# A two-layer metaformer on one core: the tiles of layer 0's experts in source order, their results stored from GpSimd's queue, and two products moved from GpSimd to VectorE

## The chip, the cores and the metric

The kernel runs on one core of a Trainium2 chip. Its engines work side by side, each through its own queue of instructions in order: TensorE (PE in the profile; its weight loads, PEld, overlap its matmuls), VectorE (DVE), ScalarE (ACT), GpSimd (POOL) and SyncE (SP), which here issues most of the DMA transfers. A profile also lists the clock that TensorE was granted. The metric is the device time of one execution in microseconds (us), as the median of several. The kernel before has three: 4149.68, 4160.04 and 4175.90 us.

## The reference

The input x is 4 images of 256 channels by 32 × 32 places, in float32. Two layers follow each other; each has a mixing half and a mixture of experts, added to x.

```
# layer 0
x = x + attention(norm_channels(x))      # 8 heads, a computed top-k, softmax, 3x3 convolution, projection
t = tokens(x)                            # 4096 tokens of 256
n = norm(t)
t = t + n + sum over the 2 chosen of 8 experts of  weight * (gelu(n @ w1[e] + b1[e]) @ w2[e] + b2[e])
# layer 1
f = norm_channels(x)
delta = softplus(f @ W_delta + b_delta);  Bm, Cm = f @ W_B, f @ W_C
h[l] = exp(delta * A) * h[l-1] + delta * f * Bm       # 16 states, in four directions over the image
x = x + (sum over the directions of (h . Cm) + f * D) / 4
t = t + the 2 chosen of 8 experts, hidden size 1024, a norm with the expert's own gain before each
```

w1 and w2 of layer 0 are 256 × 256 for each expert. The change touches layer 0's experts and the preparation (delta and delta·f) for the scans of layer 1.

## The kernel before

**Stages.** The program goes through attention (to 1905 us of the profiled execution), the norm and routing of layer 0 (to 2045), the tiles of layer 0's experts (to 2276), the scans of layer 1 (2283 to 3561), the tiles of layer 1's experts (to 4111) and the output. A planner inside the framework orders the instructions of a stage on each engine, unless the source is put under `tc.manual_schedule()`, in which case they stay in source order.

**Routing.** For each image, tokens are normed, the two experts chosen, and GpSimd scatters every token twice into rows of a DRAM tensor, slots_x0, so that each expert's rows stand together in blocks of 256. A list of 36 blocks (USUAL) covers the usual case; a branch on `more_tiles` does the rest, and the profiled execution did not take it.

**Tiles of layer 0** (`tile0`, L1480 and following). One tile is one block of 256 rows. SP reads the number of the block and of the expert into registers and loads xs (the rows, L1517), w1 and w2. VectorE copies the expert's biases out of a table that lies in SBUF (b1e L1521, b2e L1523) and computes best and wt, the choice and the weight of each row (L1525 to L1528). PE transposes the rows into tp (L1532), VectorE copies them to xe (L1534). PE multiplies into hp (L1539, two halves), ACT applies the gelu to each half, giving hid (L1540), PE multiplies into yp (L1544), and VectorE adds b2e, giving ys (L1546). For each half of ys, ACT scales it (L1548) and VectorE adds the token itself (L1549). SP's queue stores ys, 256 KB, into slots_y0 in DRAM (L1550). tp and yp have one PSUM buffer each, hp has two; ys has four buffers in SBUF.

**What goes beside the tiles.** Two chains of steps are woven in between the calls of tile0, four steps ahead of each tile: from tile 15 (FIRST) `whole(0)` and then the preparation of image 0 (`Prep.steps`), from tile 23 (SECOND) `whole(1)`. `whole(b)` gathers image b's rows out of slots_y0: GpSimd issues 16 indirect transfers (`fetched`, L1451), two to a step, 8 that write and 8 that add. After eight empty steps, `completed` transposes the rows on PE (op, L1464) and VectorE adds them to x (L1467). Because the gathers can read any row of slots_y0, and the stores write rows of it whose numbers are known only in registers, the framework makes each wait for those ahead of it in the program. Images 2 and 3 are completed later, beside the scans.

**Preparation for the scans** (`Prep.steps`). For one image: the mean over channels on PE (L1341), xm = x − mean on VectorE (L1344), its square on ACT (L1345), the variance on PE (L1353), 1/sqrt with a power on GpSimd (L1359) and four small VectorE steps to refine it (L1361 to L1364), a matmul that spreads it over the partitions (L1371), xm times it on VectorE (L1375), the matmuls for Bm and Cm (L1381) and for delta (L1407). Then the softplus for each half of the channels: Relu, Abs and Exp on ACT, three VectorE steps (L1419 to L1421), Ln on ACT (L1430), a VectorE step (L1434) and a GpSimd addition (L1435). `rest` follows with dx = delta·xm on GpSimd (L1393) and x + xm·D on VectorE (L1394). L1435 and L1393 are each issued four times for an image, on 128 × 512 elements in SBUF. Prep 0 runs beside the tiles of layer 0; Preps 1 to 3 run beside the scans.

**Scans.** 128 turns (4 images, 2 halves of the channels, 16 states). In each turn, VectorE does three scans of 128 × 1024 (L1671 forward, L1680 backward, both with decays da in PSUM; L1697 over columns, with all operands in SBUF), one small scan (L1686) and two products with Cm (L1707). GpSimd does uu = dx·Bm (L1658), a small difference (L1676) and a third product, da_c (L1691). ACT computes the decays and a flipped copy of uu, and PE sums the directions (L1666, L1701, L1708).

Of the kernel before, what the change touches and what calls it, by code (L numbers as in the profile page):

```python
# [11 lines left out]
F32 = mybir.dt.float32  # L12
# [9 lines left out]
P = 128  # L22
# [39 lines left out]
def metaformer(ctx: ExitStack, tc: tile.TileContext, t: dict, out: bass.AP):  # L62
# [86 lines left out]
    with ExitStack() as st:  # L149
# [68 lines left out]
        class Group:  # L218


            def __init__(self, b, g):
                self.b, self.g = b, g
# [1099 lines left out]
    class Prep:  # L1322
# [9 lines left out]
        def steps(self, room, psum, tag):  # L1332
# [57 lines left out]
            def rest(c):  # L1390
                for h in range(NHALF):
                    cols = ts(h, HALF)
                    nc.gpsimd.tensor_tensor(self.dx[:, c, cols], self.delta[:, c, cols], xm[:, c, cols], ALU.mult)  # L1393
                    nc.vector.scalar_tensor_tensor(x[b][:, c, cols], xm[:, c, cols], dsk[:, c : c + 1],  # L1394
                                                   x[b][:, c, cols], ALU.mult, ALU.add)
                    yield
                    yield

            behind = iter(())
            for c in range(CT):  # L1400
# [31 lines left out]
                for h in range(NHALF):  # L1432
                    dd = self.delta[:, c, ts(h, HALF)]
                    nc.vector.scalar_tensor_tensor(dd, sp[:, h], -0.5, dd, ALU.mult, ALU.add)  # L1434
                    nc.gpsimd.tensor_tensor(dd, dd, sp[:, 2 + h], ALU.add)  # L1435
                yield
                yield
                behind = rest(c)
# [34 lines left out]

    with ExitStack() as st:
        wp = st.enter_context(tc.tile_pool(name="m0_w", bufs=1))
        pb = st.enter_context(tc.tile_pool(name="m0_b", bufs=2))
# [4 lines left out]
        b1 = load(wp, "b1_0", [P, E, CT])  # L1481
        b2 = wp.tile([P, E, C], F32, tag="b2_0", name="b2_0")
        nc.sync.dma_start(b2, t["b2_0"].rearrange("e d -> (e d)").partition_broadcast(P).rearrange(
            "p (e d) -> p e d", e=E))
        tokens = [wp.tile([P, NT, W0], F32, tag=f"tok{b}", name=f"tok{b}") for b in range(B)]
        scattered = nc.alloc_semaphore("scattered")
        for b in range(B):
            d = pb.tile([P, CT, L], F32, tag="d", name="d")
            here = slot0[:, :, ts(b, NT)]
            for _ in norm(b, 0, tokens[b], pb, ps_n, "t", "t", d):  # L1490
                pass
            for _ in route(b, 0, tokens[b], here, wp.tile([P, 2560], F32, tag="numbers", name="numbers"), ps_n, "t"):
                pass

            with tc.tile_critical(name=f"scatter{b}", no_gpsimd_drain=True):
                for n in range(NT):
                    for k in range(2):
                        nc.gpsimd.indirect_dma_start(
                            out=slots_x0, out_offset=bass.IndirectOffsetOnAxis(ap=here[:, k, n : n + 1], axis=0),
                            in_=tokens[b][:, n], in_offset=None).then_inc(scattered, 16)  # L1500
                nc.gpsimd.wait_ge(scattered, 16 * 2 * NT * (b + 1))
                if b == B - 1:
                    nc.clear_and_free_semaphores([scattered])

        blocks_x, blocks_y = (a.rearrange("(k a p) c -> k p a c", a=T // P, p=P) for a in (slots_x0, slots_y0))

        def tile0(i):
            def register(k, most, engines):
                return nc.values_load(every.which[0:1, k, i : i + 1], engines=engines, min_val=0, max_val=most,
                                      skip_runtime_bounds_check_because="the minimum with that of a count")  # L1510

            block = register(1, E * BLOCKS, [mybir.EngineType.SP])
            xs = pb.tile([P, T // P, W0], F32, tag="xs", name="xs", bufs=4)
            nc.sync.dma_start(xs, blocks_x[bass.ds(block, 1)].rearrange("o p a c -> p (o a) c"))
            e = register(0, E - 1, [mybir.EngineType.SP, mybir.EngineType.DVE])
            w1 = pb.tile([P, CT, C], F32, tag="w1", name="w1", bufs=3)
            nc.sync.dma_start(w1, t["w1_0"][bass.ds(e, 1)].rearrange("o (c p) f -> p (o c) f", p=P))  # L1517
            w2 = pb.tile([P, CT, C], F32, tag="w2", name="w2", bufs=3)
            nc.sync.dma_start(w2, t["w2_0"][bass.ds(e, 1)].rearrange("o (c p) f -> p (o c) f", p=P))
            b1e = pb.tile([P, CT], F32, tag="b1e", name="b1e")  # L1520
            nc.vector.tensor_copy(b1e, b1[:, bass.ds(e, 1)].rearrange("p o c -> p (o c)"))  # L1521
            b2e = pb.tile([P, C], F32, tag="b2e", name="b2e")
            nc.vector.tensor_copy(b2e, b2[:, bass.ds(e, 1)].rearrange("p o d -> p (o d)"))  # L1523
            best = pb.tile([P, T // P], F32, tag="best", name="best")
            nc.vector.tensor_scalar(best, xs[:, :, C], every.expert[:, i : i + 1], None, ALU.is_equal)  # L1525
            wt = pb.tile([P, T // P], F32, tag="wt", name="wt")
            nc.vector.tensor_tensor(wt, best, xs[:, :, C + 1], ALU.mult)
            nc.vector.tensor_tensor(wt, wt, xs[:, :, C + 2], ALU.add)  # L1528
            tp = ps1.tile([P, CT, T], F32, tag="tp", name="tp")
            for a in range(T // P):  # L1530
                for c in range(CT):
                    nc.tensor.transpose(tp[:, c, ts(a, P)], xs[:, a, ts(c, P)], ident)  # L1532
            xe = pb.tile([P, CT, T], F32, tag="xe", name="xe")
            nc.vector.tensor_copy(xe, tp)  # L1534
            hp = ps_h.tile([P, CT, T], F32, tag="hp", name="hp")
            hid = pb.tile([P, CT, T], F32, tag="hid", name="hid")
            for f in range(CT):
                for c in range(CT):
                    nc.tensor.matmul(hp[:, f], w1[:, c, ts(f, P)], xe[:, c], start=(c == 0), stop=(c == CT - 1))  # L1539
                nc.scalar.activation(hid[:, f], hp[:, f], AF.Gelu, bias=b1e[:, f : f + 1])  # L1540
            yp = ps1.tile([P, T // P, C], F32, tag="yp", name="yp")
            for a in range(T // P):
                for f in range(CT):
                    nc.tensor.matmul(yp[:, a], hid[:, f, ts(a, P)], w2[:, f, :], start=(f == 0), stop=(f == CT - 1))  # L1544
            ys = pb.tile([P, T // P, C], F32, tag="ys", name="ys", bufs=4)
            nc.vector.tensor_tensor(ys, yp, b2e.unsqueeze(1).to_broadcast([P, T // P, C]), ALU.add)  # L1546
            for a in range(T // P):
                nc.scalar.mul(ys[:, a], ys[:, a], wt[:, a : a + 1])  # L1548
                nc.vector.scalar_tensor_tensor(ys[:, a], xs[:, a, :C], best[:, a : a + 1], ys[:, a], ALU.mult, ALU.add)  # L1549
# [9 lines left out]
        more_tiles = nc.values_load(extra[0:1, 0:1], min_val=0, max_val=1,  # L1559
                                    skip_runtime_bounds_check_because="a comparison gives 0 or 1")  # L1560
        with tc.If(more_tiles > 0):
            for i in range(USUAL, NTILE):
                tile0(i)

        def whole(b):
            y = [pb.tile([P, 4, C], F32, tag=f"y{h}", name="y", bufs=1) for h in range(NHALF)]
            yield from fetched(b, y, range(NHALF), 2)
            yield from pause(8)
            for h in range(NHALF):
                yield from completed(b, h, y[h], ps_n, "t")  # L1570

        beside = [(FIRST, chain(whole(0), preps[0].steps(room, ps_n, "t"))), (SECOND, whole(1))]
        for i in range(USUAL):
            for first_tile, steps in beside:
                if i >= first_tile:
                    for _ in range(4):
                        next(steps, None)
            tile0(i)
        for _, steps in beside:
            for _ in steps:  # L1580
                pass

    nc.vector.memset(count, 0.0)
    nc.vector.memset(done, 0.0)
# [428 lines left out]
```

## Time and the profile before

| What | Value |
|---|---|
| Time, median of 3 (us) | 4160.04 |
| The profiled execution's own time (us) | 4157.79 |
| Its span, first to last instruction (us) | 4155.8 |
| TensorE clock granted, mean | 0.88 |
| Busy share PE / DVE / ACT / POOL | 85% / 73% / 69% / 44% |
| Tiles 18 to 35 and what is beside them (us of the span) | 2127 to 2276 |
| Scans (us of the span) | 2283 to 3561 |
| Stores L1550: number, size | 36, 256 KB |
| Gathers L1451 beside the tiles: number, mean time of one on GpSimd (ns) | 32, 1281 |

The span is 2.0 us shorter than the execution's time, and the execution is 2.25 us under the median. A row of a group reads: line, engine, operation, output <- inputs, shapes, number of instructions, then busy time in us and the mean of one in ns, then the engine's idle time just before these instructions and what ended it. A row of a wait reads: the waiting engine, tile and line, then what it waited for, total us, number of times, and the longest. The busy share over the span mixes stages with different limits, so the stages are read by themselves. For a transfer, the time to landing is from the issuing instruction to the completion event in the trace.

### The profile page before, as it was taken

The page shows a single profiled execution, that of the slowest core. Times are in us where ns is not written, and L with a number is a line of the kernel's source. Part 1 is how long each engine was busy: PE and PEld are TensorE (multiplying, and loading weights), DVE is VectorE, ACT ScalarE, POOL GpSimd, SP SyncE. Part 2 cuts the span into 40 slices and gives each one's busy share as a digit, 9 for nine tenths or more (in the row PEclk, how much of TensorE's full clock was granted, in tenths as well). Part 3 has the DMA queues.
Part 4 walks back from the last instruction along what each step waited for, and adds up shares of the span by engine and source line. Part 5 has one row for each costly group of instructions (what it writes and reads, how often), then busy time and mean ns, then how long its engine had stood idle before and what let it go on. Part 6 is the DMA issues. An engine that isn't in the chain of part 4 may idle for free. (4 is left out here: it accounts for less than half of the span.)

```text
span 4155.8 us, 50303 instructions
## 1 busy us (share of the span) xinstructions
PE 3518.4 (85%) x17502; PEld 1949.6 (47%) x17502; DVE 3041.4 (73%) x5327; ACT 2847.3 (69%) x3823; POOL 1823.3 (44%) x1436
## 2 busy tenths in 40 slices
PE   8378878888888888866487999999999999999996
PEld 5144434444444444433365434443443434688885
DVE  2689899989898989883356889899899899411112
ACT  2889999999999999963235667767667677422222
POOL 0146454554455445562323666446446546221111
PEclk9568888788778877977698999999999999999997
DMA  9300093009000000001375334333333334565565
GB/s 289 92 1 1 1 263 79 1 1 306 32 1 1 11 1 1 11 1 45 118 200 167 120 104 132 102 107 114 109 100 114 118 103 136 185 186 184 188 196 184
DMA packets 280986, 426.37 MB, mean 103 GB/s; under 512 B 31889, under 2 KB 223634, under 8 KB 280594
## 3 DMA queue, kind: packets, MB, share of 16 engines
q1 hardware_dynamic: 259920, 382.66, 30.3%
q0 software_dynamic: 17024, 38.98, 3.0%
q8 instruction: 141, 2.31, 0.2%
q10 hardware_dynamic: 3778, 1.41, 0.1%
q14 instruction: 123, 1.01, 0.1%
HBM read 280.34 MB, written 142.64 MB: 102 GB/s over the span
## 5 line engine op out<-in xcount | busy, mean ns | idle before, releaser
L490 POOL TENSOR_SCALAR dr<-s_n,last 128x1024 bf16<-128x1024 f32 x256 | 732.1, 2878 | 853.9 <-DVE state L518 435.4
L406 ACT ACTIVATE junk_a<-s_n,state 128x1024 int8<-128x1024 f32 x448 | 514.6, 1149 | 25.4 <-DVE state L518 6.8
L1691 POOL TENSOR_TENSOR da_c<-prod,come 128x1024 f32<-128x1024 f32 x128 | 248.1, 1938 | 386.7 <-DVE h L1697 381.9
L410 DVE TENSOR_SCALAR_CACHE_REDUCE junk_v<-s_n,state 128x1024 int8<-128x1024 f32 x320 | 408.7, 1277 | 8.8
L1861 ACT ACTIVATE hid<-hp,b 128x256 f32<-128x256 f32 x288 | 133.7, 474 | 355.1 <-PE hp L1859 354.6
L457 DVE SCALAR_TENSOR_TENSOR w<-s_n,win 128x1024 f32<-128x1024 f32 x256 | 351.4, 1373 | 5.3
L460 DVE MAX8 win<-w 128x8 f32<-128x1024 f32 x256 | 314.5, 1228 | 8.8
L1658 POOL TENSOR_TENSOR uu<-dx,bb 128x1024 f32<-128x1024 f32 x128 | 304.9, 2382 | 1.0 <-DMA bb<-bc_d 1.0
L558 ACT ACTIVATE ex<-sT 128x1024 f32<-128x1024 f32 x256 | 247.0, 1015 | 84.5 <-PE sT L550 84.4
L1697 DVE TENSOR_TENSOR_SCAN h<-da_c,uu 128x1024 f32<-128x1024 f32 x128 | 302.8, 2366 | 0.0
L406 ACT ACTIVATE junk_a<-s_n,guess 128x1024 int8<-128x1024 f32 x256 | 294.2, 1149 | 7.4
L1671 DVE TENSOR_TENSOR_SCAN h<-da,uu 128x1024 f32<-128x1024 f32 x128 | 290.8, 2272 | 4.2 <-POOL uu L1658 4.2
L1680 DVE TENSOR_TENSOR_SCAN h<-da,uu 128x1024 f32<-128x1024 f32 x128 | 289.8, 2264 | 0.0
L568 PE MATMUL o_ps<-ex,vT 128*32 128x256 f32 x2048 | 238.1, 445 | 45.4 <-ACT ex L558 37.4
L1701 PE MATMUL hp<-h,ident 128*128 128x512 f32 x512 | 248.9, 609 | 31.1 <-DVE h L1697 30.6
L1645 ACT ACTIVATE da_c<-delta,a_log 128x1024 f32<-128x1024 f32 x128 | 268.2, 2096 | 0.2
L1859 PE MATMUL hp<-xe,w 128*128 128x256 f32 x1152 | 258.6, 381 | 6.1 <-DVE xe L1847 5.9
L1666 PE MATMUL hp<-da_c,ident 128*128 128x512 f32 x512 | 247.0, 605 | 18.2 <-POOL da_c L1691 16.3
L440 ACT COPY s_n<-sp 128x1024 f32<-128x1024 f32 x256 | 245.6, 1004 | 24.4 <-PE sp L432 12.5
L1870 DVE TENSOR_TENSOR ys<-yp,b2e 128x512 f32<-128x512 f32 x36 | 24.9, 691 | 321.1 <-PE yp L1867 321.1
L1666 PE MATMUL hp<-h,twice 128*128 128x512 f32 x512 | 243.8, 599 | 17.3 <-issue 13.4
L1659 ACT COPY uu<-uu 128x1024 f32<-128x1024 f32 x128 | 254.5, 1988 | 3.4 <-POOL uu L1658 3.4
(542 smaller groups left out, 7519.8 us busy)
## 6 DMA issues: line engine op xcount, KB each, us to landing
bb<-bc_d SPq DMA_DIRECT2D x128, 512.0 KB
cb<-bc_d SPq DMA_DIRECT2D x128, 512.0 KB
w<-in_w SPq DMA_DIRECT2D x36, 1024.0 KB
w2e<-in_w SPq DMA_DIRECT2D x36, 1024.0 KB
slots_x<-zeros SPq DMA_DIRECT2D x1, 33411.0 KB
slots_x<-zeros SPq DMA_DIRECT2D x1, 33282.0 KB
slots_y<-zeros SPq DMA_DIRECT2D x1, 33024.0 KB
w<-in_w SPq DMA_DIRECT2D x72, 256.0 KB
```

The lines of the kernel that those rows point to most:

```text
L406: nc.scalar.activation(junk, self.row(r), AF.Sign, bias=thr, scale=-1.0, accum_out=u)
L410: nc.vector.tensor_scalar(junk, self.row(r), thr, None, ALU.is_lt, ALU.add, accum_out=u)
L457: nc.vector.scalar_tensor_tensor(w, self.row(r), self.win[:, r, 0:1], self.row(r), ALU.is_gt if r < LAST_DVE else ALU.is_ge, ALU.subtract, ...
L460: nc.vector.max(out=self.win[:, r, 1:], in_=w)
L490: ins = nc.gpsimd.tensor_scalar(dr, self.row(r), self.last[:, r : r + 1], None, ALU.is_lt)
L1645: nc.scalar.activation(grid(self.da_c), cols_flipped(self.prep.delta[:, self.c]), AF.Exp, scale=self.decay)
L1658: nc.gpsimd.tensor_tensor(self.uu[:, 0], self.prep.dx[:, self.c], self.bb, ALU.mult)
L1666: nc.tensor.matmul(self.hp[h], ident if eye is None else eye, view[:, ts(h, HW // NHALF), :], start=first, stop=last)
L1671: nc.vector.tensor_tensor_scan(rows.rearrange("p r w -> p (r w)"), self.da, self.uu[:, 0], 0.0, ALU.mult, ALU.add)
L1680: nc.vector.tensor_tensor_scan(hs[:, ::-1], self.da[:, ::-1], self.uu[:, 0][:, ::-1], 0.0, ALU.mult, ALU.add)
L1697: nc.vector.tensor_tensor_scan(hs, self.da_c, self.uu[:, 1], 0.0, ALU.mult, ALU.add)
L1859: nc.tensor.matmul(hp[:, f % 2], self.w1[:, c, ts(f, P)], self.xe[:, c], start=(c == 0), stop=(c == CT - 1))
```

## The change

The change has four parts.

1. In `Prep.steps`, the addition at L1435 and the product at L1393 go from GpSimd to VectorE.
2. The tiles of layer 0 become a class with one method for each step. They are emitted under `tc.manual_schedule()`, so their order on each engine is that of the source, and so is the order of the steps beside them. Loads are issued three tiles ahead. Then, for tile i: hidden of i, store of i−1, turned (transposes and xe) of i+1, result of i, small (biases, best, wt) of i+1, load of i+3, and after that three steps of each chain that has begun.
3. The store of ys goes from SP's queue to GpSimd's queue, with the block's number read into a register of GpSimd.
4. xs has 6 buffers (before: 4), w1 and w2 have 4 (3), ys has 8 (4). `whole` gathers four transfers to a step (before: two). Norm and routing have pools of their own, which close ahead of the tiles.

```diff
-                    nc.gpsimd.tensor_tensor(self.dx[:, c, cols], self.delta[:, c, cols], xm[:, c, cols], ALU.mult)
+                    nc.vector.tensor_tensor(self.dx[:, c, cols], self.delta[:, c, cols], xm[:, c, cols], ALU.mult)
...
-                    nc.gpsimd.tensor_tensor(dd, dd, sp[:, 2 + h], ALU.add)
+                    nc.vector.tensor_tensor(dd, dd, sp[:, 2 + h], ALU.add)
...
-            xs = pb.tile([P, T // P, W0], F32, tag="xs", name="xs", bufs=4)
+                self.xs = pb.tile([P, T // P, W0], F32, tag="xs", name="xs", bufs=6)
...
-            ys = pb.tile([P, T // P, C], F32, tag="ys", name="ys", bufs=4)
+                self.ys = pb.tile([P, T // P, C], F32, tag="ys", name="ys", bufs=8)
...
-            nc.sync.dma_start(blocks_y[bass.ds(block, 1)].rearrange("o p a c -> p (o a) c"), ys)
+            def store(self):
+                for a in range(T // P):
+                    nc.scalar.mul(self.ys[:, a], self.ys[:, a], self.wt[:, a : a + 1])
+                    nc.vector.scalar_tensor_tensor(self.ys[:, a], self.xs[:, a, :C], self.best[:, a : a + 1],
+                                                   self.ys[:, a], ALU.mult, ALU.add)
+                block = self.register(1, E * BLOCKS, [mybir.EngineType.Pool])
+                nc.gpsimd.dma_start(blocks_y[bass.ds(block, 1)].rearrange("o p a c -> p (o a) c"), self.ys)
...
-            yield from fetched(b, y, range(NHALF), 2)
+            yield from fetched(b, y, range(NHALF), 4)
...
-        for i in range(USUAL):
-            for first_tile, steps in beside:
-                if i >= first_tile:
-                    for _ in range(4):
-                        next(steps, None)
-            tile0(i)
...
+        AHEAD = 3
+        with tc.manual_schedule():
+            tiles = [Tile0(i) for i in range(USUAL)]
+            for i in range(AHEAD):
+                tiles[i].load()
+            tiles[0].turned()
+            tiles[0].small()
+            for i in range(USUAL):
+                tiles[i].hidden()
+                if i > 0:
+                    tiles[i - 1].store()
+                if i + 1 < USUAL:
+                    tiles[i + 1].turned()
+                tiles[i].result()
+                if i + 1 < USUAL:
+                    tiles[i + 1].small()
+                if i + AHEAD < USUAL:
+                    tiles[i + AHEAD].load()
+                for first_tile, steps in beside:
+                    if i >= first_tile:
+                        for _ in range(3):
+                            next(steps, None)
+            tiles[-1].store()
+            for _, steps in beside:
+                for _ in steps:
+                    pass
```

More of the change, by code (lines that the diff above doesn't have):

```diff
@@ L1475, in metaformer @@
         wp = st.enter_context(tc.tile_pool(name="m0_w", bufs=1))
+        b1 = load(wp, "b1_0", [P, E, CT])
+        b2 = wp.tile([P, E, C], F32, tag="b2_0", name="b2_0")
+        nc.sync.dma_start(b2, t["b2_0"].rearrange("e d -> (e d)").partition_broadcast(P).rearrange(
+            "p (e d) -> p e d", e=E))
+        with ExitStack() as sr:
+            pr = sr.enter_context(tc.tile_pool(name="r0_w", bufs=1))
+            pd = sr.enter_context(tc.tile_pool(name="r0_b", bufs=2))
+            ps_n = sr.enter_context(tc.tile_pool(name="r0_ps", bufs=3, space=PSUM))
+            tokens = [pr.tile([P, NT, W0], F32, tag=f"tok{b}", name=f"tok{b}") for b in range(B)]
+            scattered = nc.alloc_semaphore("scattered")
+            for b in range(B):
+                d = pd.tile([P, CT, L], F32, tag="d", name="d")
+                here = slot0[:, :, ts(b, NT)]
+                for _ in norm(b, 0, tokens[b], pd, ps_n, "t", "t", d):
+                    pass
+                numbers = pr.tile([P, 1408], F32, tag="numbers", name="numbers")
+                for _ in route(b, 0, tokens[b], here, numbers, ps_n, "t"):
+                    pass
+                with tc.tile_critical(name=f"scatter{b}", no_gpsimd_drain=True):
+                    for n in range(NT):
+                        for k in range(2):
+                            nc.gpsimd.indirect_dma_start(
+                                out=slots_x0, out_offset=bass.IndirectOffsetOnAxis(ap=here[:, k, n : n + 1], axis=0),
+                                in_=tokens[b][:, n], in_offset=None).then_inc(scattered, 16)
+                    nc.gpsimd.wait_ge(scattered, 16 * 2 * NT * (b + 1))
+                    if b == B - 1:
+                        nc.clear_and_free_semaphores([scattered])
         pb = st.enter_context(tc.tile_pool(name="m0_b", bufs=2))
@@ L1479, in metaformer @@
         ps_h = st.enter_context(tc.tile_pool(name="m0_ps_h", bufs=2, space=PSUM))
[L1481 to L1503, printed above, removed]
@@ L1505, in metaformer @@
-        blocks_x, blocks_y = (a.rearrange("(k a p) c -> k p a c", a=T // P, p=P) for a in (slots_x0, slots_y0))
-        def tile0(i):
-            def register(k, most, engines):
-                return nc.values_load(every.which[0:1, k, i : i + 1], engines=engines, min_val=0, max_val=most,
-                                      skip_runtime_bounds_check_because="the minimum with that of a count")
-            block = register(1, E * BLOCKS, [mybir.EngineType.SP])
-            xs = pb.tile([P, T // P, W0], F32, tag="xs", name="xs", bufs=4)
[L1514 to L1542, printed above, removed]
-                for f in range(CT):
-                    nc.tensor.matmul(yp[:, a], hid[:, f, ts(a, P)], w2[:, f, :], start=(f == 0), stop=(f == CT - 1))
-            ys = pb.tile([P, T // P, C], F32, tag="ys", name="ys", bufs=4)
[L1546 to L1549, printed above, removed]
-            nc.sync.dma_start(blocks_y[bass.ds(block, 1)].rearrange("o p a c -> p (o a) c"), ys)
@@ new lines, in metaformer, with __init__, register, load @@
+        blocks_x, blocks_y = (a.rearrange("(k a p) c -> k p a c", a=T // P, p=P) for a in (slots_x0, slots_y0))
+        class Tile0:
+            def __init__(self, i):
+                self.i = i
+            def register(self, k, most, engines):
+                return nc.values_load(every.which[0:1, k, self.i : self.i + 1], engines=engines, min_val=0,
+                                      max_val=most,
+                                      skip_runtime_bounds_check_because="the minimum with that of a count")
+            def load(self):
+                block = self.register(1, E * BLOCKS, [mybir.EngineType.SP])
+                self.xs = pb.tile([P, T // P, W0], F32, tag="xs", name="xs", bufs=6)
+                nc.sync.dma_start(self.xs, blocks_x[bass.ds(block, 1)].rearrange("o p a c -> p (o a) c"))
+                e = self.register(0, E - 1, [mybir.EngineType.SP])
+                self.w1 = pb.tile([P, CT, C], F32, tag="w1", name="w1", bufs=4)
+                nc.sync.dma_start(self.w1, t["w1_0"][bass.ds(e, 1)].rearrange("o (c p) f -> p (o c) f", p=P))
+                self.w2 = pb.tile([P, CT, C], F32, tag="w2", name="w2", bufs=4)
+                nc.sync.dma_start(self.w2, t["w2_0"][bass.ds(e, 1)].rearrange("o (c p) f -> p (o c) f", p=P))
+            def turned(self):
+                tp = ps1.tile([P, CT, T], F32, tag="tp", name="tp")
+                for a in range(T // P):
+                    for c in range(CT):
+                        nc.tensor.transpose(tp[:, c, ts(a, P)], self.xs[:, a, ts(c, P)], ident)
+                self.xe = pb.tile([P, CT, T], F32, tag="xe", name="xe")
+                nc.vector.tensor_copy(self.xe, tp)
+            def small(self):
+                e = self.register(0, E - 1, [mybir.EngineType.DVE])
+                self.b1e = pb.tile([P, CT], F32, tag="b1e", name="b1e")
+                nc.vector.tensor_copy(self.b1e, b1[:, bass.ds(e, 1)].rearrange("p o c -> p (o c)"))
+                self.b2e = pb.tile([P, C], F32, tag="b2e", name="b2e")
+                nc.vector.tensor_copy(self.b2e, b2[:, bass.ds(e, 1)].rearrange("p o d -> p (o d)"))
+                self.best = pb.tile([P, T // P], F32, tag="best", name="best")
+                nc.vector.tensor_scalar(self.best, self.xs[:, :, C], every.expert[:, self.i : self.i + 1], None,
+                                        ALU.is_equal)
+                self.wt = pb.tile([P, T // P], F32, tag="wt", name="wt")
+                nc.vector.tensor_tensor(self.wt, self.best, self.xs[:, :, C + 1], ALU.mult)
+                nc.vector.tensor_tensor(self.wt, self.wt, self.xs[:, :, C + 2], ALU.add)
+            def hidden(self):
+                hp = ps_h.tile([P, CT, T], F32, tag="hp", name="hp")
+                self.hid = pb.tile([P, CT, T], F32, tag="hid", name="hid")
+                for f in range(CT):
+                    for c in range(CT):
+                        nc.tensor.matmul(hp[:, f], self.w1[:, c, ts(f, P)], self.xe[:, c],
+                                         start=(c == 0), stop=(c == CT - 1))
+                    nc.scalar.activation(self.hid[:, f], hp[:, f], AF.Gelu, bias=self.b1e[:, f : f + 1])
+            def result(self):
+                yp = ps1.tile([P, T // P, C], F32, tag="yp", name="yp")
+                for a in range(T // P):
+                    for f in range(CT):
+                        nc.tensor.matmul(yp[:, a], self.hid[:, f, ts(a, P)], self.w2[:, f, :],
+                                         start=(f == 0), stop=(f == CT - 1))
+                self.ys = pb.tile([P, T // P, C], F32, tag="ys", name="ys", bufs=8)
+                nc.vector.tensor_tensor(self.ys, yp, self.b2e.unsqueeze(1).to_broadcast([P, T // P, C]), ALU.add)
+            def store(self):
+                for a in range(T // P):
+                    nc.scalar.mul(self.ys[:, a], self.ys[:, a], self.wt[:, a : a + 1])
[3 more added lines that the diff above has]
+                nc.gpsimd.dma_start(blocks_y[bass.ds(block, 1)].rearrange("o p a c -> p (o a) c"), self.ys)
@@ L1552, in metaformer @@
+        more_tiles = nc.values_load(extra[0:1, 0:1], min_val=0, max_val=1,
+                                    skip_runtime_bounds_check_because="a comparison gives 0 or 1")
+        with tc.If(more_tiles > 0):
+            for i in range(USUAL, NTILE):
+                one_tile = Tile0(i)
+                for step in ("load", "turned", "small", "hidden", "result", "store"):
+                    getattr(one_tile, step)()
         preps = [Prep(0)]
@@ L1557, in room @@
             return pb.tile([P, *shape], F32, tag=tag, name=name, bufs=1 if name == "sp" else None)
[L1559 to L1562, printed above, removed]
-                tile0(i)
         def whole(b):
             y = [pb.tile([P, 4, C], F32, tag=f"y{h}", name="y", bufs=1) for h in range(NHALF)]
-            yield from fetched(b, y, range(NHALF), 2)
+            yield from fetched(b, y, range(NHALF), 4)
             yield from pause(8)
@@ L1572, in metaformer @@
         beside = [(FIRST, chain(whole(0), preps[0].steps(room, ps_n, "t"))), (SECOND, whole(1))]
-        for i in range(USUAL):
-            for first_tile, steps in beside:
-                if i >= first_tile:
-                    for _ in range(4):
-                        next(steps, None)
[L1578 to L1581, printed above, removed]
+        AHEAD = 3
[23 more added lines that the diff above has]
+                for _ in steps:
+                    pass
     nc.vector.memset(count, 0.0)
```

## The prediction

> **What bounds the kernel now.** I read the busy time by stage first (us; busy time and instruction count of each engine, then granted TensorE clock, DMA share, GB/s).
>
> ```profile
> span 4155.8 us, 50303 instructions
> ...
> 2048.00:2127.00 79.00, 73.45 (x337) 59.21 (x338) 49.74 (x151) 28.34 (x65) 0.00 (x0) 0.95 0.78 232
> 2127.00:2276.00 149.00, 112.72 (x496) 82.95 (x495) 87.02 (x222) 66.13 (x114) 53.04 (x41) 0.93 0.58 160
> 2283.00:3561.00 1278.00, 1220.06 (x3001) 533.56 (x3002) 1156.38 (x1086) 880.82 (x686) 722.77 (x488) 0.99 0.36 113
> 3561.00:4111.00 550.00, 534.98 (x2520) 455.81 (x2519) 80.73 (x225) 152.19 (x326) 85.41 (x89) 1.00 0.58 186
> ```
>
> The diff touches the first three rows only. Tiles 0 to 17 (first row) run bound by PE, 73 of 79 us: results L1546 end at 2103.82, 2108.16, 2112.51, 2116.85, one per 4.34 us, of which PE works 3.9 (hp 1.73, yp 1.73, transposes 0.44). In the second row, with gathers and Prep 0 beside the tiles, no engine is full. In the scans VectorE is busy 90%; PE's matmuls wait for scans and pad out. The second question is what the tiles wait for (us in total, times, longest):
>
> ```profile
> ACT hid L1540 <- PE hp L1539: 113.1, 56, 23.9
> ...
> POOL numbers L1451 <- DMA slots_y<-ys: 34.5, 1, 34.5
> ...
> PEld op L1464 <- DMA y<-slots_y,slot: 18.6, 9, 8.3
> DVE x L1467 <- PE op L1464: 19.8, 3, 9.9
> PE op L1464 <- DMA y<-slots_y,slot: 15.8, 9, 7.9
> ...
> POOL ln_r L1359 <- DVE ln_ve L1356: 15.3, 1, 15.3
> ```
>
> PE waits 34.4 us for gathered rows; VectorE waits behind that for op. The tile ends show where: 18 to 20 take 7.5, 16.1 and 12.6 us, tile 25 takes 19.6. Third, the scans' groups, by shape, in the scan stage (busy, mean ns), and the spread of one (min/median/max ns):
>
> ```profile
> L1697 DVE TENSOR_TENSOR_SCAN h<-da_c,uu 128x1024 f32<-128x1024 f32 x128 | 302.8, 2366 | 0.0
> L1680 DVE TENSOR_TENSOR_SCAN h<-da,uu 128x1024 f32<-128x1024 f32 x128 | 289.8, 2264 | 0.0
> ...
> L1686 DVE TENSOR_TENSOR_SCAN come<-prod,gap 128x32 f32<-128x32 f32 x128 | 35.5, 277 | 0.0
> L1435 POOL TENSOR_TENSOR delta<-delta,sp 128x512 f32<-128x512 f32 x12 | 28.8, 2416 | 5.3 <-DVE delta L1434 5.3
> L1393 POOL TENSOR_TENSOR dx<-delta,xm 128x512 f32<-128x512 f32 x12 | 16.0, 1330 | 0.2
> L1394 DVE SCALAR_TENSOR_TENSOR x<-xm,dskip,x 128x512 f32<-128x512 f32 x12 | 8.7, 722 | 0.0
> L1375 DVE TENSOR_TENSOR xm<-xm,ln_rb 128x512 f32<-128x512 f32 x12 | 7.6, 675 | 2.4 <-PE ln_rb L1371 2.4
> ```
> ```profile
> L1697 DVE TENSOR_TENSOR_SCAN h<-da_c,uu x128: 2258/2269/3641, 2287.8 to 3556.6; 128x1024 f32<-128x1024 f32 x128
> ```
>
> L1697 and L1680 do equal work, yet L1697 has a mean 0.1 us higher. Its long cases stand exactly beside L1435 or L1393 on GpSimd: with an L1435 it takes 3.37 instead of 2.27, with an L1393 3.64, and the small scan L1686 takes 1.58 to 1.95 instead of 0.22.
>
> **The products (L1393, L1435).** Eight of each Prep's move to VectorE. VectorE pays 24 in the scans by the nearest rows, a product L1375 0.68 and L1394 0.72: I take 0.65 (back to back, pairs take 1.28), 15.6 us, 5.2 a Prep. It gets back the stretching: 3.1 us beside Prep 1 (1.11, 0.51, 1.10, 0.41) and 8.0 beside each of Preps 2 and 3 (1.09, 1.37, 1.36, 1.10, 1.37, 1.72), in all 19.1; the means agree: 128 × (2.366 − 2.264) + 128 × (0.277 − 0.216) = 20.9. Beside Prep 1 GpSimd is short too: the turn at 2466.5 takes 12.9 us, since GpSimd is busy 11.4 of it and the outputs L1707 idle 4.2; fewer products give back some 3.5. So −1.5, −2.8, −2.8: **scans −7**. Bounds: +8 where VectorE's queue gives half the stall back, +15.6 where the stretching isn't GpSimd's, −10 where the pairs of L1435 also free the next turn.
>
> The skill's page SBUF — State Buffer, section Who interferes with whom, says that a VectorE instruction with two SBUF inputs and a GpSimd instruction share a port pair under an exclusive lock. That fits L1697 beside L1435; taken as a rule it would also stretch L1680 beside GpSimd's L1658 (2.38 us each turn, same shape), and L1680's maximum is 2.274, its decays coming from PSUM.
>
> **The order of the tiles.** Source order puts tile i−1's scaling (ACT mul, VectorE L1549, two each) between gelu(i) and xe(i+1). From start of hp(i): 1.73 matmuls, 0.26 to the second gelu, 0.37 to the first mul, 1.33 for mul and L1549 to the start of xe, xe 0.69, 0.1 to hp(i+1): **4.48** a tile against 4.34. 36 tiles: 161 us against 156, +5, and 2 at the start.
>
> The work beside the tiles: before, the stage from 2048.5 to VectorE's last operation at 2274 is 225.5, so 69 us are stalls. After, the order is fixed, and I add what each iteration waits beyond 4.48. Image 0's gathers start at tile 15, four to a step, three steps to a tile (before: two to a step, four steps): 12 stand on GpSimd's queue behind store 14, then 4 and store 15, and a store waits for all gathers ahead of it to land, since both touch slots_y. With 8 first gathers at 1.26 and 8 adding ones at 1.84, from before's issues, and 3.4 for the landing of store 14 (below), op (L1464) stands on PE in tiles 19 and 20 before its rows have landed, and hp and yp of these tiles are queued behind it: +6, +7. Then +3.5, +1, +5 in tiles 21 to 23 (mean 1.73 and squares 1.23 ahead of tile work on PE and ACT). Then pow L1359: before it ran at 2172.20 between the images' gathers. Now 12 of image 1's gathers (1.3 to 1.8 each, some 18 us) and store 23 stand ahead of it on GpSimd. VectorE's rr (L1361) waits for pow, and behind rr on VectorE are the next tile's L1549, xe and ys, for which PE waits: 15 to 17 us, and with rb and xn behind it +18.5 at tile 25. Tiles 26 to 29: +2, +4, +1.6, +1.6. Tiles 30 to 32: softplus in order on ACT (two table loads of 1.28 each way, Exp 0.63, Ln 1.06) and eight products of 0.65 on VectorE: +9.5, +6.8, +4.2; then +1. Sum 71, near the 69 of before: the planner's stalls are replaced, not removed. The slow cases of b2e (3.43 us for 0.29, beside L1435) go; they lie within these waits, and I count nothing for them. End: 2048.5 + 2 + 161 + 71, and 4 for the last tile's scaling: 2286.5, **+12.5**.
>
> **Stores from GpSimd's queue.** A store is 256 KB. SP's landed 2.2 to 4.1 us after issue. GpSimd's nearest direct row is L1941, of the same size: 0.54 us of GpSimd for each issue, landing after 2.3 to 2.5 us with empty queues and 5.3 to 6.3 with eight 1 MB loads moving. On GpSimd each store waits for the landing of the one before it, with gathers and pow queued behind, and the eighth mul after it waits for its buffer. So the chain costs nothing while the landing, counted from the start of the issue, stays below 4.48; beyond that, every tile pays the excess. In the tiles DMA is 58 to 83% busy. I take 3.4, between the idle row and the busy one and nearer to the idle, because a tile's loads are 0.77 MB and not eight at once; at 2.6 the stage gains 3.5 through earlier gathers, at 5.5 it loses 36 × 1.02 = 37. The load of a_log behind the last landing comes bare: +1.
>
> The skill's page DMA: Bandwidth & Descriptors, section Anatomy of one DMA — SWDGE (gpsimd) path, gives about 2.0 us plus bytes over 436 GB/s. For 256 KB this is 2.6 us, an estimate from that page; with it the stage would gain 3.5 against my sum.
>
> **Buffers and pools**: zero. Loads of xs were waited for only at the start (PE 24.5 us in two waits), so more buffers and an SP queue without stores hide nothing more; GpSimd's new register read lies in its idle time. The order of norm and routing on PE, VectorE and ACT is unchanged.
>
> Sum: +12.5 − 7 + 1 = +6.5 on the profiled 4157.8: 4164.3; the median of the shown runs is 2.25 above that execution, so about **4166**.
>
> **Rivals.** (a) *Faster*: gathers issued early and three steps a tile hide the stalls: tiles 15 to 35 at 5.5 us on average where my sum has 4.48 + 71/21 = 7.9: 50 off the stage, 4116. For: PE works 112.7 of 149 us. Against: pow's queue position. (b) *Slower*: the store chain on GpSimd is longer than a tile. It decides from a landing of 4.48 us. For: L1941 with loads took 5.3 to 6.3, and DMA is 83% busy in the early tiles. Price: 36 × (5.6 − 4.48) = 40 on my sum, 4206. Against: 0.77 MB of loads a tile, not 8 MB. (c) The products' stretching isn't GpSimd's: +15.6 instead of −7, 4189. (d) The program's source order is what the planner found anyway: 4158.
>
> **Chances.** Forecast 0.5 and (c) 0.1, (d) 0.1, all within 1%; (a) 0.1; (b) 0.2, three quarters of it over 1%. 1% (41.6 us) is about what a measurement of this kernel can tell from no change. Faster by over 1%: 0.09; same 0.75; slower 0.16. The range leaves out (a)'s far half and (b)'s: 4130 to 4208.
>
> **What would show it.** Right: L1697's maximum falls to 2.3 and L1686's to 0.23; results of early tiles 4.4 to 4.6 us apart; one VectorE wait of over 10 us for pow; op waits for gathers near tiles 19 and 20. Wrong: L1697 still over 3 us (c); POOL stores waiting for stores, or the ACT mul waiting for a store landing (b); no wait above 5 us (a).

## The result, and the profile after

The changed kernel takes 4212.43 us (median of 4 runs, 4198.34 to 4224.51) against 4155.99 for the kernel before (4 runs, 4149.68 to 4175.90). The ratio is 1.0124, with a 95% interval of 1.0093 to 1.0154: slower by 56 us. I had said 4166, within 1%, and a range up to 4208. The median lies 4 us above that range.

The profiled execution took 4224.51 us, 12 over its median, with a span of 4222.8. Five distances in the two traces show where the 67.0 us between the spans lie:

| Stretch of the trace (us) | before | after | difference |
|---|---|---|---|
| Start to the first norm of routing (L1253), code not in the diff | 1905.5 | 1923.1 | +17.6 |
| From there to the first transposes of the tiles | 143.0 | 138.2 | −4.8 |
| First transposes of the tiles to the first scan (L1671, now L1716) | 234.3 | 292.4 | +58.1 |
| First to last of these scans | 1267.4 | 1262.6 | −4.8 |
| Last of these scans to the end | 605.6 | 606.4 | +0.8 |

The first two rows together vary from 2029 to 2061 us in the runs of this study, whose code there is the same or nearly so. So their difference is no more than runs differ by themselves. The tiles and the scans are what the change touched.

The stages of the changed kernel, in the view by windows (us; busy time and count of PE, PEld, DVE, ACT, POOL; clock, DMA share, GB/s):

```profile
2061.00:2163.00 102.00, 84.36 (x365) 61.59 (x366) 50.73 (x161) 31.80 (x71) 15.96 (x20) 0.95 0.67 208
2163.00:2340.00 177.00, 123.24 (x468) 89.51 (x467) 80.74 (x214) 57.98 (x104) 52.52 (x49) 0.83 0.43 117
2353.00:3627.00 1274.00, 1222.86 (x3001) 534.64 (x3002) 1151.70 (x1110) 880.88 (x687) 678.48 (x463) 0.99 0.36 112
```

The first row has the first 18 tiles, 0 to 17. Before, these run to 2134, and not to 2127, as the prediction and the table ahead of it have it; by the view of the kernel before, PE is busy 80 of 86 us there:

```profile
2048.00:2134.00 86.00, 80.26 (x371) 64.86 (x372) 54.31 (x165) 30.56 (x70) 5.00 (x6) 0.96 0.79 235
```

Now it is busy 84 of 102. So these tiles are no longer bound by PE, and for most of them no gather has begun (the first is issued at 2156.5). From the second to the 18th the results L1568 end 5.35 us apart, where it was mostly 4.34. The waits of this stage (2048 to 2340) say for what:

```profile
PEld hp L1557 <- ACT hid L1559: 55.0, 34, 6.6
PE hp L1557 <- ACT hid L1559: 40.4, 34, 6.2
...
DVE ln_rr L1361 <- POOL ln_r L1359: 11.9, 1, 11.9
...
PEld op L1464 <- DMA y<-slots_y,slot: 9.5, 5, 5.6
...
POOL slots_y L1576 <- DMA slots_y<-ys: 8.6, 3, 3.3
...
PE op L1464 <- DMA y<-slots_y,slot: 7.9, 4, 5.2
```

hp waits for hid in 34 of 36 tiles. The rows of PEld and PE cover the same idle time: 55.0 us in all, not the sum of the two. Before, the same pair of lines stood lower in the table of waits, and I passed over it:

```profile
PEld hp L1539 <- ACT hid L1540: 15.4, 24, 3.5
...
PE hp L1539 <- ACT hid L1540: 8.8, 21, 3.1
```

One early tile in the timeline (start, duration, engine, line, operation; in brackets the idle time before it and its releaser) shows the mechanism:

```profile
2108.46 0.68 DVE L1537 COPY xe<-tp 128x512 f32<-128x512 f32 x1
...
2109.20 1.13 PE L1557 MATMUL hp<-xe,w 128*128 128x256 f32 x4 [0.31 <-DVE xe L1537]
...
2110.42 0.47 ACT L1559 ACTIVATE hid<-hp,b1e 128x256 f32<-128x256 f32 x1 [2.39 <-DVE wt L1549]
...
2110.94 1.13 PE L1557 MATMUL hp<-xe,w 128*128 128x256 f32 x4 [0.61 <-ACT hid L1559]
2111.70 0.57 PEld L1535 LDWEIGHTS tp<-ident,xs 128*128 128x128 f32 x4
2111.91 0.60 PE L1535 MATMUL tp<-ident,xs 128*128 128x128 f32 x4
2112.11 0.47 ACT L1559 ACTIVATE hid<-hp,b1e 128x256 f32<-128x256 f32 x1 [1.22 <-PE hp L1557]
...
2112.48 0.89 ACT L1572 ACTIVATE ys<-ys,wt 128x256 f32<-128x256 f32 x2
2113.01 0.88 DVE L1573 SCALAR_TENSOR_TENSOR ys<-xs,best,ys 128x256 f32<-128x256 f32 x2 [2.47 <-ACT ys L1572]
2113.81 0.68 DVE L1537 COPY xe<-tp 128x512 f32<-128x512 f32 x1
```

hp is one PSUM tile with two halves. The first half's matmuls run at 2109.20, its gelu at 2110.42, and only when that has ended do the second half's matmuls start, at 2110.94. From the start of one half to the other is 1.74 us, where I had counted on PE going straight on. In source order nothing of PE stands between the halves. Before, the planner had put matmuls of the neighbouring tiles there, and 0.42 us of idle time was left in most early tiles. The releaser named for the first gelu (wt) is only the last event seen; the matmuls of hp's first half end at 2109.20 + 1.13 = 2110.33, as close to it.

The scans went the way that was worked out, 4.8 us down for the 7 foretold. The column scan, its spread (min/median/max ns) and its group beside that of the small scan:

```profile
L1742 DVE TENSOR_TENSOR_SCAN h<-da_c,uu x128: 2259/2268/2296, 2358.8 to 3622.8; 128x1024 f32<-128x1024 f32 x128
```
```profile
L1742 DVE TENSOR_TENSOR_SCAN h<-da_c,uu 128x1024 f32<-128x1024 f32 x128 | 290.9, 2273 | 0.0
...
L1731 DVE TENSOR_TENSOR_SCAN come<-prod,gap 128x32 f32<-128x32 f32 x128 | 28.0, 219 | 0.0
L1435 DVE TENSOR_TENSOR delta<-delta,sp 128x512 f32<-128x512 f32 x12 | 8.3, 693 | 0.8
L1393 DVE TENSOR_TENSOR dx<-delta,xm 128x512 f32<-128x512 f32 x12 | 8.0, 668 | 0.0
```

The maximum of 3641 ns is now 2296, and the small scan's mean fell from 277 to 219. VectorE pays 16.3 us for the 24 products and gets 11.9 + 7.5 = 19.4 back in these two groups. From profile to profile the stretch of the scans moves by some us: it is 1258.8 to 1264.9 in the eleven that have the products on VectorE, 1267.4 and 1268.4 in the two that have them on GpSimd.

### The profile page after: what moved, and what is told of

Same layout as the page of the kernel before. It is cut to its first block, busy times and chain, and to the rows that moved or that the text cites. A ratio compares the mean times of both kernels' runs of the same rounds, so it can differ in the third digit from the quotient of the medians.

```text
span 4222.8 us, 50316 instructions
## 1 busy us (share of the span) xinstructions
PE 3551.4 (84%) x17502; PEld 1968.0 (47%) x17502; DVE 3034.3 (72%) x5359; ACT 2840.5 (67%) x3819; POOL 1793.8 (42%) x1440
## 3 DMA queue, kind: packets, MB, share of 16 engines
q1 hardware_dynamic: 250128, 373.22, 29.2%
## 5 line engine op out<-in xcount | busy, mean ns | idle before, releaser
L1703 POOL TENSOR_TENSOR uu<-dx,bb 128x1024 f32<-128x1024 f32 x128 | 304.1, 2376 | 3.3 <-DMA bb<-bc_d 3.2
L1716 DVE TENSOR_TENSOR_SCAN h<-da,uu 128x1024 f32<-128x1024 f32 x128 | 290.8, 2272 | 4.2 <-ACT da L1698 4.2
L1742 DVE TENSOR_TENSOR_SCAN h<-da_c,uu 128x1024 f32<-128x1024 f32 x128 | 290.9, 2273 | 0.0
L1725 DVE TENSOR_TENSOR_SCAN h<-da,uu 128x1024 f32<-128x1024 f32 x128 | 289.9, 2264 | 0.0
L1912 PE MATMUL yp<-w2e,hid 128*128 128x256 f32 x1152 | 255.9, 379 | 0.0
```

The source lines that it names most:

```text
L1703: nc.gpsimd.tensor_tensor(self.uu[:, 0], self.prep.dx[:, self.c], self.bb, ALU.mult)
L1716: nc.vector.tensor_tensor_scan(rows.rearrange("p r w -> p (r w)"), self.da, self.uu[:, 0], 0.0, ALU.mult, ALU.add)
L1725: nc.vector.tensor_tensor_scan(hs[:, ::-1], self.da[:, ::-1], self.uu[:, 0][:, ::-1], 0.0, ALU.mult, ALU.add)
L1742: nc.vector.tensor_tensor_scan(hs, self.da_c, self.uu[:, 1], 0.0, ALU.mult, ALU.add)
L1912: nc.tensor.matmul(yp[:, a], self.hid[:, f, ts(a, P)], self.w2[:, f, :], start=(f == 0), stop=(f == NF - 1))
```

## The experiments

Times to compare are those of each group of runs, with the kernel before run beside them. "Stage" is the stretch from the first transposes to the first scan: 234.3 before, 292.4 after. "Period" is the distance of early tile results. Both are read from one profiled execution of each kernel. How far such a reading repeats can be seen where two kernels have the same tiles: from the first tile result to the last it is 263.5 and 264.7 us in the changed kernel and with the products on GpSimd again, 236.2 and 236.0 with two hp tiles and with a_log loaded early as well.

### Two tiles for hp

```diff
-                hp = ps_h.tile([P, CT, T], F32, tag="hp", name="hp")
...
                 for f in range(CT):
+                    hp = ps_h.tile([P, T], F32, tag="hp", name="hp")
```

The rest of the lines follow, and the pool has three buffers instead of two.

> The changed kernel, except that each half of hp (one for each gelu) is a PSUM tile of its own, three buffers, where both halves were one tile of two buffers. My theory: the period of the early tiles is 5.35 us in place of my 4.48 because the second half's matmuls wait for the gelu of the first half, which reads the same tile. Then the period falls to 4.4 to 4.6 us, TensorE's waits for hid at hp are gone, and the tiles (from the first transposes to the first scan, 292.5 us) lose 25 to 45 us: a time of 4165 to 4190. Rival, the store chain on GpSimd: the period stays above 5 us and the time within 10 of 4212.

Measured: 4185.19 us (before: 4161.29), ratio 1.0046 (1.0027 to 1.0064). The period is 4.47, the stage 263.2, 29.2 less. In the early tiles hp waits only for xe, at most 0.7 us at a time:

```profile
PEld hp L1557 <- DVE xe L1537: 11.5, 16, 0.7
...
PE hp L1557 <- DVE xe L1537: 5.0, 16, 0.3
```

So the shared tile is the cause of the longer period, and 4.47 is the 4.48 of my chain without that wait. The stage is still 28.9 us longer than before, all of it after the 18th tile: the first 18 take 85.3 us, before 85.7. Whether the framework watches the tile as a whole or the place of both halves in PSUM, this run doesn't tell apart.

### Stores on SP's queue

```diff
-                nc.gpsimd.dma_start(blocks_y[bass.ds(block, 1)].rearrange("o p a c -> p (o a) c"), self.ys)
+                nc.sync.dma_start(blocks_y[bass.ds(block, 1)].rearrange("o p a c -> p (o a) c"), self.ys)
```

> The changed kernel, except that the stores of ys go through SP's queue again. My theory: a store lands 3.1 to 3.5 us after its issue, under the period of 5.35, so the chain of stores sets nothing; the early period stays 5.35 and the stage (292.5 us) changes by less than 10. Rival, the chain of stores on GpSimd is the cause of the loss: the stage falls by 30 or more and the early period to under 4.6.

Measured: 4213.02 us, one run. Period 5.36, stage 293.6. So the chain of stores doesn't set the period of 5.35. In the changed kernel the stores of the first 15 tiles go out 0.3 us after VectorE's last step for them (0.7 for the first). Counted as in the prediction, from the start of the issue to the last completion event, they land after 3.4 to 4.6 us (median 3.9) while tiles run at full rate, and after 2.5 to 2.7 for most of the later ones. The 3.1 to 3.5 of the expectation come near the first of a store's 16 completion events (2.8 to 3.6), not the last. On SP's queue the same 15 stores land after 2.2 to 2.5.

That the stage is the same hides a trade. Here the loads of xs stand on SP's queue behind stores that wait for the gathers, and PE waits 19.4 us for them in three waits beside the tiles; the wait of op for gathered rows, 9.5 in the changed kernel, is gone.

### The products on GpSimd again

```diff
-                    nc.vector.tensor_tensor(dd, dd, sp[:, 2 + h], ALU.add)
+                    nc.gpsimd.tensor_tensor(dd, dd, sp[:, 2 + h], ALU.add)
```

The same for L1393; all else as in the changed kernel.

> The changed kernel, except that the two products of the preparation (L1393, L1435) are on GpSimd again. My theory, stretching by GpSimd: the longest L1742 scan comes back to over 3.3 us, the longest L1731 to over 1.5, and the stretch from the first to the last L1716 rises from 1262.6 to 1266 to 1271. Rival, the products cost VectorE more than the stretching: it falls to 1250 to 1258. The tiles' stage changes by less than 10 us.

Measured: 4214.08 us, one run. The scans take 1268.4 us, 5.8 more, and the long ones are back:

```profile
L1742 DVE TENSOR_TENSOR_SCAN h<-da_c,uu x128: 2257/2268/3649, 2342.9 to 3612.7; 128x1024 f32<-128x1024 f32 x128
```

The longest L1731 is 1.94 us. The stage is 292.9, 0.5 more, which is within what two profiles differ by: no cost of the products beside the tiles is seen on either engine.

### The products alone, on the kernel before

The two lines L1393 and L1435 of the kernel before go to VectorE, and nothing else.

> The kernel before, with only the two products moved to VectorE. My theory: the stretch from the first to the last L1671 falls from 1267.4 to 1259 to 1265 us, the scans beside Preps are no longer stretched, and the whole is 0 to 12 us faster than before, about 4150. Rival: the products cost VectorE 15.6 us and give nothing back, so the stretch rises to 1275 to 1285.

Measured: 4146.77 us against 4161.29, ratio 0.9966 (0.9950 to 0.9983). That is 14.5 us, a little more than I expected. The scans take 1259.7, 7.7 less than before; the longest column scan is 2.29 us. This part of the change is a gain by itself, and in the change it was covered by the loss in the tiles.

### a_log loaded early

With two hp tiles; the load stands beside that of dskip (L1318). In the trace it is issued at 1917.1 us, ahead of routing and not, as the expectation says, ahead of attention.

```diff
+    am = load(sw, "a_log", [P, CT, NS])
...
-        am = load(wp, "a_log", [P, CT, NS])
```

> The kernel with two hp tiles (263.2 us from the first transposes to the first scan), and the load of a_log is issued ahead of attention instead of behind the last tile. In the changed kernel the first scan starts 17.5 us after the last L1568, where the kernel before takes 10.3; my theory is that a_log's load, which stands behind the last store's landing, is the cause. Then that distance falls to 10 to 13 us and the stage to 256 to 260. Rival, the store's landing itself or bb's load sets it: the distance stays above 16.

Measured: the distance is 12.74 us, was 17.38; the stage 258.2, 5.0 less; 4170.65 us, one run. With the load, the Exp L1650 and the scaling L1651 went to 1920.8 and 1921.1 us, so the edit tells what load, Exp and scaling cost together. In the changed kernel the load is issued at 2342.65, behind the last store's landing, its Exp L1650 starts at 2347.34, and the first decays at 2349.62. Before, da_c was computed at 2277.66, 3.7 us after the last store's issue.

### Image 1's gathers behind the power

With two hp tiles; image 1's chain begins four tiles later.

```diff
-        beside = [(FIRST, chain(whole(0), preps[0].steps(room, ps_n, "t"))), (SECOND, whole(1))]
+        beside = [(FIRST, chain(whole(0), preps[0].steps(room, ps_n, "t"))), (SECOND + 4, whole(1))]
```

> The kernel with two hp tiles, and the chain of image 1 begins at tile 27 instead of 23, so that its gathers stand behind the power L1359 on GpSimd and not ahead of it. My theory: VectorE's wait for the power (22.2 us at ln_rr) falls under 4, and the stage goes from 263.2 to 240 to 252. Rival, the steps beside the tiles cost what they cost, wherever they stand: the stall moves to another tile and the stage stays within 5 of 263.

Measured: 4153.45 us, one run; stage 241.6, 21.6 less. The wait for the power, with two hp tiles and then with this edit as well (the line with its idle time and what ended it):

```profile
  POOL ln_r L1359: 22.2, 1
```
```profile
  POOL ln_r L1359: 1.9, 1
```

The stall didn't move: it went. The place of 12 gathers on GpSimd's queue ahead of one small operation cost some 21 us, through the queue of VectorE behind rr.

### All three, and the transposes ahead of the store

```diff
+                if i + 1 < USUAL:
+                    tiles[i + 1].turned()
                 if i > 0:
                     tiles[i - 1].store()
-                if i + 1 < USUAL:
-                    tiles[i + 1].turned()
```

> The kernel with two hp tiles, with a_log loaded early and image 1's chain from tile 27 as in the two others, and the transposes of tile i+1 emitted ahead of tile i-1's store, so that xe does not stand behind L1573 on VectorE. If the three gains add up: early period 4.2 to 4.35 instead of 4.47, stage 230 to 245, time 4145 to 4165, so no slower than the kernel before. If the chain through L1573 did not set the period, it stays 4.47.

Measured: 4145.30 us against 4157.81, ratio 0.9974 (0.9951 to 0.9997). The period is 3.89, TensorE's own 3.9, and lower than I expected; the stage is 236.3. The first 18 tiles take 75.1 us, some 10 less than with the other mendings, but tile 20 now takes 26.2 where it took 14.6. (The expectations of the last runs count these slow tiles one too low. They also add up the rows of PEld and PE, which cover the same idle time: their 51.8 and 39.2 us of waiting for rows are 27.1 and 21.5.) TensorE waits at tiles 20 and 21 for image 0's rows, which come no earlier:

```profile
POOL slots_y L1577 <- DMA slots_y<-ys: 28.2, 8, 4.4
PEld op L1465 <- DMA y<-slots_y,slot: 27.1, 8, 15.0
...
PE op L1465 <- DMA y<-slots_y,slot: 24.7, 8, 14.6
```

The first line shows what holds them back: GpSimd's stores wait for the landing of the one before. They go out 4.73 us apart where the tiles end 3.89 apart, each some 0.6 us after the landing before it. ys has eight buffers, so the tiles run on, but store 14 goes out 12.5 us after VectorE is done with it, and the gathers stand behind it. They begin 82.7 us after the first transposes, and 80.4 with image 1's chain moved alone, at a period of 4.47.

### The planner's kernel with products and two hp tiles

The kernel before with the two products on VectorE and the split of hp; the order is the planner's and the stores are SP's.

> The kernel before (planner's order, stores on SP) with the two products on VectorE and two hp tiles. Before, TensorE worked 3.9 of each 4.34 us and waited 15.4 and 8.8 us for hid at hp, which the planner had partly filled with other matmuls. Theory: the early period falls to 4.0 to 4.3, the stage by 0 to 15 us, the time to 4130 to 4150. Rival: the planner had hidden it all, period 4.34, time within 5 of the kernel with the products alone, 4147.

Measured: **4134.54 us** against 4157.81, ratio 0.9942 (0.9921 to 0.9963): faster than both kernels, and the lowest ratio of all that ran. Period mostly 4.08 to 4.21, stage 221.6. So the wait for hid was not wholly hidden in the kernel before either.

### Later use of the gathered rows

In `whole`, `pause(20)` instead of `pause(8)`; in the source-order kernel with all mendings also four steps beside each tile instead of three.

> The source-order kernel with all three mendings (stage 236.3 us, tiles 19 and 20 at 26 and 13 us, TensorE waiting 51.8 us for gathered rows at op), with 20 empty steps instead of 8 between an image's gathers and their use, and four steps beside each tile instead of three, so that the chains still end with the tiles. My theory: the wait of op for rows falls under 10 us and the stage to 205 to 225. Rival: the work after it is pushed into fewer tiles and the end takes the gain back: stage 230 to 245.

Measured: 4149.57 us against 4151.27, ratio 1.0007 (0.9986 to 1.0027); stage 239.6. The wait of op for rows falls from 27.1 to 13.4 us, not under 10. The tiles up to 21 now run at 3.89, and those from 22 on take 18, 6.5, 7.8, 9.1, 17.6 and so on. The rival holds: the work is pushed into fewer tiles and nothing is gained.

> The planner's kernel with the products on VectorE and two hp tiles (stage 221.6 us, tile 18 at 20.8), with 20 empty steps instead of 8. Theory: the wait of op for rows (39.2 us) falls under 15, the stage to 200 to 218, the time to 4115 to 4130. Rival: the planner places op by its own estimates, so empty steps in the source change nothing: stage 218 to 226.

Measured: 4140.26 us against 4151.27, ratio 0.9970 (0.9953 to 0.9987), stage 228.9. The wait of op for rows is gone, as the theory had it, so the planner does follow the empty steps; but the stage gets longer by 7.3, outside both ranges. Which stalls took its place I did not follow up.

### Stores on SP at the short period

> The source-order kernel with all three mendings, stores through SP's queue. Its period is 3.89 us, and a store lands 3.1 to 3.5 us after its issue when tiles run at full rate. Theory: the store chain on GpSimd still fits the period, so the stage (236.3) stays within 10. Rival: the chain binds at this rate and its backlog delays the gathers; then the stage falls by 15 or more and tile 19's 26 us shrinks.

Measured: 4164.06 us, one run; stage 243.0, 6.7 longer; tile 18 takes 24.2 and tile 19 12.5. The stage stays within 10, as the theory said, but for another reason. On SP's queue the stores go out 3.90 us apart (4.73 on GpSimd's), and the gathers begin 71.1 us after the first transposes (82.7). So the chain on GpSimd does bind at a period of 3.89 and does delay the gathers, as the rival had it. The stage isn't shorter because SP has a stall of its own: store 15 waits there for the gathers, the loads of xs stand behind it, and PE waits 18.0 and 6.0 us for them at tiles 18 and 19. The op wait is gone; instead this line stands in the view (the longest, 23.9, is the start of the stage):

```profile
PE tp L1536 <- DMA xs<-slots_x: 62.3, 5, 23.9
```

What the late stores alone cost the kernel with all mendings, no run here separates.

## Why the prediction was wrong in size

**The step that failed is the chain of one tile**, "1.73 matmuls, 0.26 to the second gelu". It let hp's two halves follow each other on PE. The second waits for the gelu of the first, so from hp's start to the second gelu it is 2.91 us (2109.20 to 2112.11), not 1.99, and the rest of my chain holds: 0.37 to the mul, 1.33 to xe, 0.68, and 0.06 to hp, 5.35 in sum. Over 36 tiles 0.87 makes 31 us; two hp tiles gave 29.2. The step failed in its mechanism, not only in its size: a wait was left out.

**The stalls beside the tiles** I put at 71 us over the period (the terms as listed make 71.7). By tile ends 18 to 35 they were 173.0 − 18 × 5.35 = 76.7. The sum came near by luck: tiles 19 and 20 cost little, and op stalled at tile 21 instead, which took 18.1 us with 9.2 of waiting for rows. The last four gathers stand behind store 15 (2178.7) and are issued from 2183.1; I had that store behind them. The wait for the power was 11.9, against 15 to 17; at the period that I had assumed, it was 22.2, above my bound. There, with two hp tiles, the stalls are 160.6 − 18 × 4.47 = 80.1, 9 over my 71, and the stage came out 28.9 longer than before, where I had 12.5 and 1 for a_log. What I compared with was also set a little high: of the 69 us of stalls before, some lay in the first 18 tiles (85.7 − 18 × 4.34 = 7.6). And the 34.4 us that PE was said to wait for gathered rows before are 18.6: I added two rows for the same idle time.

**The tail** I put at +1. It is 7.2 (17.52 less 10.33), and 4.6 of that is a_log's load with the Exp and the VectorE step behind it, by the experiment. I had priced part of the transfer and neither of these; the rest is not resolved.

**The products** were right: −7 predicted, −4.8 in the changed kernel, −7.7 alone; the stretch is GpSimd's, shown both ways. In the kernel before, the ten column scans that run beside an L1435 or an L1393 take 3.36 to 3.64 us, and the other 118 at most 2.29. The Trainium skill's page SBUF — State Buffer, section Who interferes with whom, fits these scans: with GpSimd's two products gone, no column scan is above 2.30 us. The backward scan (L1680, now L1725) is no exception to it, as the prediction had it: the page speaks of two inputs in SBUF, and this scan has one, its decays being in PSUM. It runs beside L1703 in 127 turns and never takes over 2.27 us. One small scan, both of whose inputs are in SBUF, still meets an L1703 and takes 0.66 us instead of 0.22.

**The stores**: 3.4 us assumed, 3.4 to 4.6 measured at full rate (median 3.9). Where one store waits for another, some 0.6 more pass between a landing and the next issue, which my limit of 4.48 left out. So a link of the chain takes some 4.5 us at the median, an estimate from these two. That costs nothing at 5.35; with two hp tiles, at 4.47, the stores are 4.53 apart and up to 2.2 us late; at 3.89 they fall behind. And then not every tile pays, as I had it, but the gathers behind the stores. Rival (b) gave the right sign and nearly the price (4206) by luck: in the changed kernel the chain did not bind. The Trainium skill's page DMA: Bandwidth & Descriptors, section Anatomy of one DMA — SWDGE (gpsimd) path, leads to an estimate of 2.6 us; most stores of the stalled tiles come near it (2.5 to 2.7), those of the dense ones take 3.4 to 4.6.

**What the signs said.** The profile after was to show early results "4.4 to 4.6 us apart"; 5.35 refuted that at once. "Op waits near tiles 19 and 20" came at tile 21, and the wait for the power came as said. Stores waiting for stores, the sign of (b), show 8.6 us in the changed kernel, in three waits, all after the first gathers; no operation of a tile is seen waiting for a store to land.

The whole: 58.1 us more in the stage, of which 29.2 are hp's shared tile, 21.6 the power behind the gathers (as seen with hp mended), 5.0 a_log's load and what follows it; 2.3 are left over. In the stage the effects depend on each other, so this is one order of taking them apart.

## What to carry to other kernels

When a planner's order is replaced by source order, list for every wait that the old trace shows (here hp for hid, 15.4 us in all, which became 55.0) what the planner had put in its place: in source order that cover is gone, and here the wait was paid in 34 of 36 tiles. A PSUM tile written and read in two parts is worth trying as two tiles: as one, here, the writer of the second part waited for the reader of the first. Count the idle time of PE and PEld once where both wait for the same thing. On an engine with few but urgent small operations, count what long transfers are queued ahead of them; and try the parts of a change one by one, since a gain (here 0.34%) can hide in a loss.

## What the runs showed that I had not expected

- Emitting the transposes of the next tile ahead of the store takes the period from 4.47 to 3.89 us, all of it PE's work. I expected 4.2 at best. In that trace the two gelus of a tile run from 2096.89, in 0.85 us, beside the transposes, and no wait of PE is left between early tiles.
- That gain, 10 us over 18 tiles, was fully given back at the first use of gathered rows. At that rate the stores on GpSimd's queue fall behind, and the gathers stand behind the stores.
- Before the tiles, executions of the same code differ by up to 32 us (2029 to 2061 us to the first transposes). Differences of a few us between kernels were read from the distances within the tiles and scans.
